# Turning matrices on the way through a DMA: gate and expert tiles of a two-layer graph kernel

## The chip, the core and the metric

The kernel runs on one core of one Trainium2 chip. The metric is the device time of one launch in microseconds (us), the median over several runs. The engines are called by what they do: TensorE (PE in the profile; its weight loads are PEld), VectorE (DVE), ScalarE (ACT), GpSimd (POOL) and SyncE (SP), which here only issues DMAs.

## The reference, cut to what matters

There are 128 graphs of 64 nodes, so 8192 tokens of 256 features, and two layers. Each layer is a graph step and then a mixture of experts, each with a layer norm ahead and a residual sum behind. The change touches the mixture of layer 0 alone:

```python
H = jax.nn.gelu(xf @ W1 + b1, approximate=False)        # 8192 x 1024
probs = jax.nn.softmax((H @ Wg + bg) / TEMP, axis=-1)   # 8 experts
assign = jnp.argmax(probs, axis=-1)
for e in range(Wd.shape[0]):                            # Wd[e]: 1024 x 256
    y = H @ Wd[e] + bd[e]
    out = out + jnp.where(assign == e, probs[:, e] * y, 0.0)
```

So each token needs the product with one of eight matrices, that of its best expert. Layer 1 holds an attention over each graph, a second mixture of four experts and a gate that is computed over a graph of 1,048,576 edges.

## The kernel before

Tokens stand in 64 tiles of 128 and in 16 groups of four tiles (`GR = 4`, 512 tokens). Three stages of layer 0 matter here.

**The gate.** `gated(g)` works on one group. It normalises the four tiles (`z`, L734), turns them on TensorE (L746, evicted by ScalarE at L747), and then `hidden` makes eight tiles hT of 128 hidden features x 512 tokens: two matmuls (L498) and a gelu on ScalarE (L501) each. hT has features on the partitions. The logits come from hT by a further product (L765, L769, L774); softmax, best expert and the rank of each token within its expert's list are small VectorE operations. The token's place is `pos` = expert x 8192 + rank.

To sort the tokens by expert, their gelu rows must go to `hrows` in device memory, one row of 1024 floats for each token. So each hT is turned back by four transposes on TensorE (`turned`, L755) and copied by ScalarE into `rows` (L756), which has tokens on the partitions; this runs `BEHIND = 4` steps after the gelu. At the end of the group four indirect DMAs on GpSimd's queue (L818) scatter the rows, 128 rows of 4 KB each. `rows` is a single buffer; hT tiles come from the pool `bh` with ten buffers.

**The early tiles.** `early_slots` works on 8 tiles of 128 sorted rows that are complete before the gate ends. Each is loaded from `hrows` (L900, two DMAs of 256 KB), turned by eight transposes (L911) and copied (L913), multiplied with its expert's `wd` (L932), and stored.

**The slots.** `slots` works through 60 such tiles. For each: a load of 512 KB (`hin`, L1238, two tiles ahead), eight transposes (L1247) and two copies on ScalarE (L1250) into `hTt`, eight products (L1265) that sum into one PSUM tile, the bias on VectorE (L1273), and a store to `yrows` (L1274). The expert's number is read from a table into registers, and picks `wd` and the bias row.

What runs beside them sets the order. The instruction streams of a part (two groups) are mixed by `mix` in the proportion of their steps, and each engine then has one fixed order of instructions. Beside the gate run the graph step of the groups ahead (L645 to L693) and, on VectorE, `keys.collect`: 16 chunks of the edge list, each loaded by SP (L279), searched for its largest keys by repeated max and replace (L296, L297), and written back by SP (L316). Source, destination and key tiles of a chunk have one buffer each. Beside the slots run on VectorE the later part of that sorting (`steps`, L373 to L451) and the counting of edges (`counts`: comparisons at L203, matmuls at L341), and `back_early`, which gathers finished rows on GpSimd's queue (L1193). All plain loads and stores of these stages are issued by SP, whose queue is in order.

Of the kernel before, what the change touches and what calls it, by code (L numbers as in the profile page):

```python
# [10 lines left out]
F32 = mybir.dt.float32  # L11
I32 = mybir.dt.int32
U32 = mybir.dt.uint32
U8 = mybir.dt.uint8
BF16 = mybir.dt.bfloat16
# [19 lines left out]
EARLY = 8  # L35
BACKED = 3 * PART
# [33 lines left out]
BEHIND = 4  # L70
# [14 lines left out]
def kernel(  # L85
# [102 lines left out]
    hrows = dram.tile([E0 * N, FD], F32, name="hrows")  # L188
    yrows = dram.tile([(NSLOT + EARLY) * P, D], F32, name="yrows")
    psel = const.tile([P, NT], F32, name="psel")  # L190
    row_y = const.tile([P, NT], I32, name="row_y")
    off = const.tile([P, NT, 64], U8, name="off")
    cnt = const.tile([P, NT], F32, name="cnt")
# [261 lines left out]
    with tc.tile_pool(name="w0", bufs=1, reuse_waits="tile") as w0, tc.tile_pool(name="kp", bufs=1, reuse_waits="tile") as kp:  # L455
# [15 lines left out]
        slot_e = w0.tile([P, NSLOT], I32, name="slot_e")  # L471
        slot_row = w0.tile([P, NSLOT], I32, name="slot_row")
# [13 lines left out]
        with tc.tile_pool(name="bg1", bufs=1, reuse_waits="tile") as bg1, tc.tile_pool(  # L486
# [19 lines left out]
            with tc.tile_pool(name="b2", bufs=1, reuse_waits="tile") as b2, tc.tile_pool(  # L506
# [199 lines left out]
                of_row = bg1.tile([P, 1], I32, name="of_row")  # L706
                nc.gpsimd.iota(of_row, pattern=[[0, 1]], base=0, channel_multiplier=1)
# [17 lines left out]
                def gated(g):  # L725
# [24 lines left out]
                    rows = b2.tile([P, GR, FD], F32, name="rows")  # L750

                    def turned(q):
                        th = psb.tile([P, GR * P], F32, name="tz")
                        for k in range(GR):
                            nc.tensor.transpose(th[:, k * P : k * P + P], hTs[q][:, k * P : k * P + P], ident)  # L755
                        S.copy(rows[:, :, q * P : q * P + P], th.rearrange("p (k n) -> p k n", k=GR))  # L756

                    for q, _ in enumerate(hidden(zT, hTs)):
                        if q >= BEHIND:
                            turned(q - BEHIND)  # L760
                        yield
# [8 lines left out]
                    turned(NH - BEHIND)  # L770
# [4 lines left out]
                    turned(NH - BEHIND + 1)  # L775
# [8 lines left out]
                    turned(NH - BEHIND + 2)  # L784
# [10 lines left out]
                    turned(NH - BEHIND + 3)  # L795
# [19 lines left out]
                    for k in range(GR):  # L815
                        t = GR * g + k
                        alone(
                            nc.gpsimd.indirect_dma_start(  # L818
                                hrows, bass.IndirectOffsetOnAxis(ap=pos[:, t : t + 1], axis=0), rows[:, k, :], None
                            )  # L820
                        )
# [55 lines left out]
                def early_slots():  # L877

                    _, rows_at = nc.values_load_multi_w_load_instructions(
                        early_row,  # L880
                        engines=(mybir.EngineType.SP,),
                        min_val=0,
                        max_val=E0 * N - P,
                        skip_runtime_bounds_check_because=why,
                    )
                    _, ex = nc.values_load_multi_w_load_instructions(
                        early_e,
                        engines=(mybir.EngineType.SP, mybir.EngineType.PE),
                        min_val=0,
                        max_val=E0 - 1,  # L890
                        skip_runtime_bounds_check_because=why,
                    )
                    loaded, turned_ = {}, {}

                    def load(t):

                        loaded[t] = []
                        for i in range(0, FD, GR * P):
                            h = bh.tile([P, GR * P], F32, name="hT")
                            got = nc.sync.dma_start(h, hrows[bass.ds(rows_at[t], P), i : i + GR * P])  # L900
                            for other in sends[-PART * GR :]:
                                tc.declare_no_dep(got.ins, other, reason="rows of an early tile were sent before")
                            loaded[t].append(h)

                    def turn(t):

                        turned_[t] = []
                        for h in loaded.pop(t):
                            th = psb.tile([P, GR * P], F32, name="tz")
                            for k in range(GR):  # L910
                                nc.tensor.transpose(th[:, k * P : k * P + P], h[:, k * P : k * P + P], ident)  # L911
                            hT = bh.tile([P, GR * P], F32, name="hT")
                            S.copy(hT, th)  # L913
                            turned_[t].append(hT)

                    load(0)
                    load(1)
                    turn(0)
                    yield
                    for t in range(EARLY):  # L920
                        if t + 2 < EARLY:
                            load(t + 2)
                        if t + 2 == EARLY:
                            y_last = bh.tile([P, GR * P], F32, name="hT")[:, 0:D]
                        if t + 1 < EARLY:
                            turn(t + 1)
                        hT = turned_.pop(t)
                        bd = b2.tile([P, D], F32, name=f"z{2 + t % 2}")
                        nc.sync.dma_start(bd, f0_bd[bass.ds(ex[t], 1), :].to_broadcast([P, D]))
                        py = psb.tile([P, GR * P], F32, name="ph")[:, 0:D]  # L930
                        for q in range(NH):
                            nc.tensor.matmul(  # L932
                                py,
                                hT[q // GR][:, q % GR * P : q % GR * P + P],
                                wd[:, bass.ds(ex[t], 1), q, :].rearrange("p e f -> p (e f)"),
                                start=(q == 0),
                                stop=(q == NH - 1),
                            )
                        y = y_last if t == EARLY - 1 else b2.tile([P, D], F32, name=f"z{t % 2}")
                        V.tensor_tensor(y, py, bd, ALU.add)  # L940
                        queue = nc.sync if t < EARLY - 2 else nc.gpsimd
                        queue.dma_start(yrows[(NSLOT + t) * P : (NSLOT + t + 1) * P, :], y)
                        yield
# [10 lines left out]
                for i in range(n_parts + 2):  # L954
# [18 lines left out]
                    if i == 1:  # L973
                        with tc.issue_after(first_made[-1]):
                            for e in range(E0):
                                nc.sync.dma_start(
                                    hrows[e * N : e * N + P, :].rearrange("p (k f) -> p k f", f=P),
                                    none.unsqueeze(1).to_broadcast([P, FD // P, P]),
# [177 lines left out]
        if True:  # L1156
            with tc.tile_pool(name="bs", bufs=3, reuse_waits="tile") as bs, tc.tile_pool(
                name="bt", bufs=2, reuse_waits="tile"
            ) as bt, tc.tile_pool(name="be", bufs=2, reuse_waits="tile") as be, tc.tile_pool(name="bz", bufs=3, reuse_waits="tile") as bz, tc.tile_pool(
                name="psy", bufs=2, space=PSUM, reuse_waits="tile"  # L1160
            ) as psy, tc.tile_pool(name="pst", bufs=4, space=PSUM, reuse_waits="tile") as pst, ExitStack() as of_keys:
# [44 lines left out]
                def slots(first, end):  # L1206

                    found, loaded, turned = {}, {}, {}

                    def load(t):  # L1210

                        if t % GR == 0:
# [10 lines left out]
                                engines=(mybir.EngineType.SP, mybir.EngineType.PE),  # L1223
# [6 lines left out]
                                engines=(mybir.EngineType.SP,),  # L1230
# [6 lines left out]
                        h = loaded[t] = bz.tile([P, FD], F32, name="hin")  # L1237
                        nc.sync.dma_start(h, hrows[bass.ds(found[t][0], P), :])  # L1238

                    def turn(t):  # L1240

                        h = loaded.pop(t)
                        hT = turned[t] = bt.tile([P, NH, P], F32, name="hTt")
                        for i in range(0, NH, GR):
                            th = pst.tile([P, GR * P], F32, name="th")
                            for k in range(GR):
                                nc.tensor.transpose(  # L1247
                                    th[:, k * P : k * P + P], h[:, (i + k) * P : (i + k) * P + P], ident
                                )
                            S.copy(hT[:, i : i + GR, :].rearrange("p q n -> p (q n)"), th)  # L1250

                    for t in range(first, min(first + 2, end)):
                        load(t)
                    turn(first)
                    for t in range(first, end):
                        if t + 2 < end:
                            load(t + 2)
                        if t + 1 < end:
                            turn(t + 1)
                        (_, e, to), hT = found.pop(t), turned.pop(t)  # L1260
                        bd = bs.tile([P, D], F32, name="bd")
                        nc.sync.dma_start(bd, f0_bd[bass.ds(e, 1), :].to_broadcast([P, D]))
# [11 lines left out]
                        stored = nc.sync.dma_start(yrows[bass.ds(to, P), :], y)  # L1274
# [1209 lines left out]
```

## Time and profile before

| | |
|---|---|
| median of 15 runs | 2006.2 us (1998.43 to 2014.45) |
| the profiled execution | 2005.77 us |
| its span in the profile | 2004.0 us |
| busy: TensorE / VectorE / ScalarE / GpSimd | 1874.6 / 1354.3 / 949.1 / 454.1 us |
| mean granted TensorE clock | 0.983 |
| DMA: moved, mean rate | 284.91 MB, 142 GB/s |

The span runs from the first to the last record of the profile; the time of the execution is 1.8 us longer. A busy share is an average over stages with different limits, so the table of stages in the prediction counts for more than this one. Float32 matmuls are recorded as several instructions each (960 for the 480 products of the slots), and overlap: the busy time of a group is the time that it covers, which is less than its number times its mean length.

### The profile page before, as it was taken

To read this page: it belongs to the slowest core of one execution; us is meant where nothing else is said; L and a number is where in the kernel's file an instruction comes from. 1 tells how busy PE (TensorE), PEld (TensorE's weight loads), DVE (VectorE), ACT (ScalarE), POOL (GpSimd) and SP (SyncE) were. 2 spreads that over 40 slices of the span, in tenths; PEclk is the share of its full clock that TensorE was granted. 3 is DMA by queue.
4 is the path that set the end of the run, shared out by engine and by line. 5 is a ranking of instruction groups with operands and counts; after the bars stand their busy time and mean duration, and the time that the engine had idled before them with its cause. 6 is when DMAs were issued, how large, how long until landed. Compare 5 with 4: busy or idle time off the path is not lost. (4 is left out here: it accounts for less than half of the span.)

```text
span 2004.0 us, 32697 instructions
## 1 busy us (share of the span) xinstructions
PE 1874.6 (94%) x10609; PEld 1329.8 (66%) x10609; DVE 1354.3 (68%) x4535; ACT 949.1 (47%) x1740; POOL 454.1 (23%) x467
## 2 busy tenths in 40 slices
PE   7888989989999999999978999999999989999999
PEld 5444544444557888888646666656666658888876
DVE  6789988972456899998498656847778443234435
ACT  4867667676663222122567766323333323333332
POOL 3010111011111011120231100016666543312223
PEclk9999999999999999999979999999999999999999
DMA  9752322323425555455224211662222358888833
GB/s 295 204 166 83 119 83 100 105 87 115 147 82 177 174 181 175 156 175 165 61 69 143 68 51 55 203 169 57 59 54 60 90 179 286 279 252 272 278 119 95
DMA packets 243552, 284.91 MB, mean 142 GB/s; under 512 B 55920, under 2 KB 195312, under 8 KB 243376
## 3 DMA queue, kind: packets, MB, share of 16 engines
q1 hardware_dynamic: 209392, 221.96, 35.9%
q0 software_dynamic: 23136, 60.48, 9.4%
q8 instruction: 89, 1.46, 0.3%
q10 hardware_dynamic: 10848, 0.30, 0.3%
q14 instruction: 87, 0.71, 0.1%
HBM read 159.40 MB, written 123.18 MB: 141 GB/s over the span
## 5 line engine op out<-in xcount | busy, mean ns | idle before, releaser
L498 PE MATMUL ph<-zT,w 128*128 128x512 f32 x512 | 250.3, 610 | 6.0 <-ACT zT L747 4.9
L1265 PE MATMUL py<-wd,hTt 128*128 x960 | 217.9, 380 | 0.7 <-ACT hTt L1250 0.7
L1878 POOL DMA_INDIRECT got<-tsrc,esrc x144 | 156.9, 1090 | 174.4 <-DVE esrc L1849 77.3
L1265 PEld LDWEIGHTS py<-wd,hTt 128*128 128x128 f32 x960 | 178.5, 191 | 22.9 <-ACT hTt L1250 0.9
L1415 PE MATMUL py<-w,hT 128*128 128x256 f32 x736 | 175.4, 390 | 8.7 <-DVE td L2237 4.9
L1250 ACT COPY hTt<-th 128x512 f32<-128x512 f32 x120 | 64.4, 589 | 240.2 <-PE th L1247 227.4
L1405 PE MATMUL ph<-zT,w 128*128 128x512 f32 x368 | 169.9, 604 | 1.3 <-issue 1.2
L1415 PEld LDWEIGHTS py<-w,hT 128*128 128x128 f32 x736 | 139.0, 194 | 36.5 <-issue 12.1
L498 PEld LDWEIGHTS ph<-zT,w 128*128 128x128 f32 x512 | 92.6, 194 | 98.5 <-issue 79.5
L2363 ACT ACTIVATE hT<-ph,b1e 128x256 f32<-128x256 f32 x152 | 72.1, 474 | 179.2 <-PE ph L2359 98.0
L1409 ACT ACTIVATE hT<-ph,b 128x512 f32<-128x512 f32 x92 | 63.1, 688 | 171.1 <-PE ph L1405 135.4
L2359 PE MATMUL ph<-zTp,w1e 128*128 128x256 f32 x608 | 140.0, 384 | 4.4 <-DMA w1e<-in_L_ffn_W_dram 4.4
L818 POOL DMA_INDIRECT hrows<-rows,pos x64 | 64.7, 1011 | 338.2 <-issue 185.5
L2380 DVE TENSOR_TENSOR y<-py,b2e 128x256 f32<-128x256 f32 x76 | 32.3, 424 | 160.6 <-PE py L2372 149.2
L2372 PE MATMUL py<-w,hT 128*128 x608 | 137.8, 379 | 1.7 <-issue 1.7
L2359 PEld LDWEIGHTS ph<-zTp,w1e 128*128 128x128 f32 x608 | 117.2, 193 | 21.0 <-issue 4.6
L501 ACT ACTIVATE hT<-ph,b 128x512 f32<-128x512 f32 x128 | 88.1, 688 | 83.5 <-PE ph L498 75.4
L660 PE MATMUL pre<-wd 128*128 128x512 f32 x256 | 124.5, 604 | 1.9 <-ACT wd L646 1.3
L2372 PEld LDWEIGHTS py<-w,hT 128*128 128x128 f32 x608 | 112.6, 190 | 15.8 <-issue 2.1
L1405 PEld LDWEIGHTS ph<-zT,w 128*128 128x128 f32 x368 | 67.8, 191 | 69.4 <-issue 68.6
L2393 POOL DMA_INDIRECT back<-yslots,place x64 | 64.3, 1005 | 169.3 <-ACT hT L1409 49.3
L755 PEld LDWEIGHTS tz<-ident,hT 128*128 128x128 f32 x512 | 62.2, 143 | 53.4 <-issue 42.0
(499 smaller groups left out, 3881.8 us busy)
## 6 DMA issues: line engine op xcount, KB each, us to landing
hin<-hrows SPq DMA_DIRECT2D x60, 512.0 KB
w1e<-in_L_ffn_W_dram SPq DMA_DIRECT2D x38, 512.0 KB
yin<-ystore SPq DMA_DIRECT2D x24, 512.0 KB
yrows<-none SPq DMA_DIRECT2D x10, 1024.0 KB
zslots<-none SPq DMA_DIRECT2D x38, 256.0 KB
zin<-zslots SPq DMA_DIRECT2D x38, 256.0 KB
yslots<-y SPq DMA_DIRECT2D x76, 128.0 KB
ystore<-y SPq DMA_DIRECT2D x72, 128.0 KB
```

The costliest lines, as they stand in the source:

```text
L498: nc.tensor.matmul(ph, w1[:, c, q * P : q * P + P], zT[:, c, :], start=(c == 0), stop=(c == 1))
L501: gelus.append(S.activation(hT, ph, AF.Gelu, bias=b1[:, q : q + 1]).ins)
L660: nc.tensor.matmul(pre, xnT[:, c, n * P : n * P + P], wcat[:, c, :], start=(c == 0), stop=(c == 1),)
L818: nc.gpsimd.indirect_dma_start(hrows, bass.IndirectOffsetOnAxis(ap=pos[:, t : t + 1], axis=0), rows[:, k, :], None)
L1250: S.copy(hT[:, i : i + GR, :].rearrange("p q n -> p (q n)"), th)
L1265: nc.tensor.matmul(py, hT[:, q, :], wd[:, bass.ds(e, 1), q, :].rearrange("p e f -> p (e f)"), start=(q == 0), stop=(q == NH - 1),)
L1405: nc.tensor.matmul(ph, w1[:, e, c, q * P : q * P + P], zT[:, c, :], start=(c == 0), stop=(c == 1))
L1415: nc.tensor.matmul(py, hTs[q][:, k * P : k * P + P], w2[:, e, q, :], start=(q == 0), stop=(q == NH1 - 1))
L1878: nc.gpsimd.indirect_dma_start(got, None, tsrc, bass.IndirectOffsetOnAxis(ap=esrc[:, b, at : at + 1], axis=0))
L2359: nc.tensor.matmul(ph, w1e[:, c, q * P : q * P + P], zT[:, c, :], start=(c == 0), stop=(c == 1))
L2363: pace[:] = [S, S.activation(hT, ph, AF.Gelu, bias=b1e[:, q : q + 1]).ins]
L2372: nc.tensor.matmul(py, hTs[q][:, k * P : k * P + P], w2[:, e, q, :].rearrange("p e f -> p (e f)"), start=(q == 0), stop=(q == NH1 - 1),)
```

## The change

The turns leave TensorE and ScalarE and become transposing DMAs on SP's queue. Such a DMA takes two-byte elements, so a row of floats is handled as two rows: one of the lower halves of its 1024 floats, one of the upper halves, 2 KB each. `hrows` has twice as many rows of 1024 two-byte elements. In the gate a transposing DMA (128 x 1024 two-byte elements, 256 KB) takes each hT as soon as its gelu is done to `rows`, in which each partition now holds half rows. Half row number 2 x place + (0 or 1) must be known on the partition that holds it: two small matmuls with a matrix that spreads 64 tokens over 128 partitions, and one VectorE operation, make that index. The sends become eight per group with 2 KB rows instead of four with 4 KB rows. Early tiles and slots are loaded by a transposing DMA from `hrows` straight into the layout that the products need: two of 256 KB for an early tile, one of 512 KB for a slot, now three slots ahead (`AHEAD = 3`). Bias loads and result stores of these two stages move from SP's queue (and for the last two early tiles from GpSimd's) to ScalarE's queue. The PSUM tiles that held the turns are gone; `py` gets four buffers instead of two.

```diff
-    hrows = dram.tile([E0 * N, FD], F32, name="hrows")
+    hrows = dram.tile([E0 * N * 2, FD], U16, name="hrows")
...
-                    rows = b2.tile([P, GR, FD], F32, name="rows")
-
-                    def turned(q):
-                        th = psb.tile([P, GR * P], F32, name="tz")
-                        for k in range(GR):
-                            nc.tensor.transpose(th[:, k * P : k * P + P], hTs[q][:, k * P : k * P + P], ident)
-                        S.copy(rows[:, :, q * P : q * P + P], th.rearrange("p (k n) -> p k n", k=GR))
+                    rows = b2.tile([P, 2 * GR, FD], U16, name="rows")
 
                     for q, _ in enumerate(hidden(zT, hTs)):
-                        if q >= BEHIND:
-                            turned(q - BEHIND)
+                        nc.sync.dma_start_transpose(rows[:, :, q * P : q * P + P], hTs[q].bitcast(U16))
                         yield
...
-                    for k in range(GR):
-                        t = GR * g + k
+                    p2 = psg0.tile([P, GR * P], F32, name="ms")[:, 0 : 2 * GR].rearrange("p (k h) -> p k h", h=2)
+                    for j in range(2):
+                        nc.tensor.matmul(p2[:, :, j], spread_pos[j], m, start=True, stop=True)
+                    at = pr.rearrange("p k e -> p (k e)")[:, 0 : 2 * GR].bitcast(I32)
+                    V.tensor_scalar(at, p2.rearrange("p k h -> p (k h)"), 2.0, odd, ALU.mult, ALU.add)
+                    yield
+                    for j in range(2 * GR):
                         alone(
                             nc.gpsimd.indirect_dma_start(
-                                hrows, bass.IndirectOffsetOnAxis(ap=pos[:, t : t + 1], axis=0), rows[:, k, :], None
+                                hrows, bass.IndirectOffsetOnAxis(ap=at[:, j : j + 1], axis=0), rows[:, j, :], None
                             )
                         )
...
-                            got = nc.sync.dma_start(h, hrows[bass.ds(rows_at[t], P), i : i + GR * P])
-                            for other in sends[-PART * GR :]:
+                            got = nc.sync.dma_start_transpose(
+                                h.bitcast(U16).rearrange("p (q r) -> p q r", q=GR),
+                                hrows[bass.ds(rows_at[t] * 2, 2 * P), i : i + GR * P],
+                            )
+                            for other in sends[-PART * GR * 2 :]:
...
-                        nc.sync.dma_start(bd, f0_bd[bass.ds(ex[t], 1), :].to_broadcast([P, D]))
+                        nc.scalar.dma_start(bd, f0_bd[bass.ds(ex[t], 1), :].to_broadcast([P, D]))
...
-                        queue = nc.sync if t < EARLY - 2 else nc.gpsimd
-                        queue.dma_start(yrows[(NSLOT + t) * P : (NSLOT + t + 1) * P, :], y)
+                        nc.scalar.dma_start(yrows[(NSLOT + t) * P : (NSLOT + t + 1) * P, :], y)
...
-                        h = loaded[t] = bz.tile([P, FD], F32, name="hin")
-                        nc.sync.dma_start(h, hrows[bass.ds(found[t][0], P), :])
...
+                        hT = loaded[t] = bt.tile([P, NH, P], F32, name="hTt")
+                        nc.sync.dma_start_transpose(
+                            hT.rearrange("p q r -> p (q r)").bitcast(U16).rearrange("p (q r) -> p q r", q=NH),
+                            hrows[bass.ds(found[t][0] * 2, 2 * P), :],
+                        )
+
+                    def bias(t):
+
+                        bd = biases[t] = bs.tile([P, D], F32, name="bd")
+                        nc.scalar.dma_start(bd, f0_bd[bass.ds(found[t][1], 1), :].to_broadcast([P, D]))
...
                         y = bs.tile([P, D], F32, name="y")
                         add_bd = V.tensor_tensor(y, py, bd, ALU.add).ins
-                        stored = nc.sync.dma_start(yrows[bass.ds(to, P), :], y)
+                        stored = nc.scalar.dma_start(yrows[bass.ds(to, P), :], y)
```

## The prediction

> **What bounds the kernel now.** I read the busy shares first, then a table of the stages that the change touches, then groups and waits, then the DMA queues. The stage borders are the starts of z (L734) on ScalarE, two groups to a row: 70.7 to 619.7 us is the gate of layer 0 (16 groups), 619.7 to 663 the early tiles, 663 to 966.5 the 60 slots. Columns: length, busy us (instructions) by engine, granted clock, DMA share, GB/s.
>
> ```profile
> core 0: us, PE busy (x) PEld busy (x) DVE busy (x) ACT busy (x) POOL busy (x), PEclk, DMA share, GB/s
> 70.70:141.60 70.90, 61.37 (x229) 32.63 (x229) 62.16 (x218) 51.44 (x90) 5.36 (x6) 0.95 0.65 195
> 212.20:283.60 71.40, 66.35 (x285) 35.81 (x284) 64.43 (x239) 51.49 (x89) 10.03 (x12) 1.00 0.28 96
> 431.80:498.60 66.80, 61.98 (x261) 33.07 (x261) 21.42 (x92) 47.49 (x81) 8.78 (x8) 1.00 0.28 95
> 498.60:555.70 57.10, 53.49 (x316) 29.56 (x316) 24.97 (x100) 36.88 (x61) 8.11 (x8) 1.00 0.42 148
> 619.70:663.00 43.30, 40.44 (x325) 34.74 (x324) 34.22 (x154) 8.99 (x17) 4.97 (x6) 1.00 0.57 183
> 663.00:966.50 303.50, 299.46 (x2593) 268.03 (x2593) 268.94 (x683) 64.44 (x120) 39.34 (x25) 0.99 0.53 168
> ```
>
> TensorE is the bound everywhere, at 0.92 of the time in the gate and 0.99 in the slots. But VectorE is right behind it (64 of 71 us; 269 of 303.5), until its edge chunks run out near 440 us: what TensorE saves, VectorE may keep.
>
> ```profile
> L1265 PE MATMUL py<-wd,hTt 128*128 x960 | 217.9, 380 | 0.7 <-ACT hTt L1250 0.7
> L1250 ACT COPY hTt<-th 128x512 f32<-128x512 f32 x120 | 64.4, 589 | 240.2 <-PE th L1247 227.4
> L755 PE MATMUL tz<-ident,hT x512: 272/273/331, 94.9 to 617.9; 128*128 128x128 f32 x171
> L1247 PE MATMUL th<-ident,hin x480: 272/273/451, 663.1 to 959.3; 128*128 128x128 f32 x160
> ```
>
> These are the turns. One takes 273 ns, but they overlap: asked for alone, L755 covers 78.96 us (154 ns each) and L1247 64.96 us (135 ns).
>
> ```profile
> SPq L316 <- DVE key L314: 114.4, 9, 17.5
> DVE key L283 <- DMA left<-key: 14.3, 9, 3.4
> L818 POOL DMA_INDIRECT hrows<-rows,pos x64: 957/964/1507, 128.8 to 630.6; - x64
> ```
>
> SP's queue waits for VectorE's chunks, up to 17.5 us at a time, and VectorE waits for SP's left stores: `key` has one buffer.
>
> ```profile
> q1 hardware_dynamic: 209392, 221.96, 35.9%
> q10 hardware_dynamic: 10848, 0.30, 0.3%
> ```
>
> No row shows a transposing DMA; these two give its bounds.
>
> **The price of a transposing DMA (T, for 256 KB).** At the least, the plain rate: the slots move 168 GB/s at a share of 0.53, so 317 GB/s when full, T = 0.83 us. At the most, the rate of the smallest packets: 0.3% of 16 engines over 2004 us is 96 us for 10,848 packets, 8.9 ns for 28 bytes, 50 GB/s over 16 engines, T = 5.2 us. Between: q1's packets take 55 ns for 1060 bytes (35.9% x 16 x 2004 / 209,392). A line through both points gives 19 ns for 256 bytes, which is one block of 128 two-byte elements, the run that both sides of this transfer have; 1024 of these on 16 engines are T = 1.2 us. I take 1.2, as the nearest by run length, and 2.4 us for the 512 KB of a slot. The Trainium skill, "DMA: Bandwidth & Descriptors", Latency and other measured facts, gives 261 GB/s for a DMA transpose with a non-contiguous middle dimension; by that T would be 1.0 us and the sum below about 6 us lower (estimate). Against the change speaks "VectorE: DVE Perf Modes", The three transpose paths: 1309 ns by DMA for 128x128 two-byte elements against 390 on TensorE; were that a rate and not one transfer's latency, T would be 8 x 1.309 = 10.5 us and the kernel would take some 4200 us (estimate). No run here shows either yet.
>
> **Gate.** Removed: 512 transposes, 79.0 us of TensorE, and 128 copies into rows, 74.0 us of ScalarE (L756). Added: 128 transposing DMAs on SP, 64 more sends on POOL (128 of half the size), and per group two small matmuls and one small VectorE operation (a 128x4 to 128x32 operation takes 0.17 us: under 0.5 us per group in all, hidden in the idle tenth).
>
> Groups 0 and 1 (70.9 us): the DMA share is 0.65 and VectorE has 62 us; I give them 4. Groups 2 to 11 take 357.0 us. TensorE: their windows hold 326.6 us, less 48.7 of turns, so 27.8 per group; at today's fill of 0.91, 30.5. VectorE: the instruction order puts 13 edge chunks between groups 1 and 11 where before they lay between 1 and 9. A chunk is 15.3 us in the timeline (348.66 to 364.4 less one foreign operation), other work 9 per group: (13 x 15.3 + 10 x 9) / 10 = 28.9, at the same fill 31.7. I take 31.2 per group, 312 us: **45 less**. Groups 12 to 15 have little VectorE work; the copies of their gate logits on ScalarE (L769) lie 29.3, 25.4, 25.4 and 28.3 us apart, 108.4. Here a new loop binds. `rows` has one buffer, and the first transposing DMA of a group waits until all eight sends of the group before have landed. Sends start 1.27 us apart on POOL: 10.2 us; a landing is about 2.8 us (the left store that VectorE waits for, 345.8 to 348.7); then 8T, and a landing again: 15.8 + 8T, 25.4 us at T = 1.2. So 102 instead of 108: I take **8 less**, with the overlap of the last landing. In groups 2 to 11 the same loop hides under 31.2 us while T is under 1.9.
>
> SP now carries the transposing DMAs between edge loads and left stores. If one waits for a chunk (17.5 us at worst), the ones behind it wait; hT has 10 buffers and a group uses 9, so TensorE has a group's slack, and what is late is the sends, which have 5.8 us per group. The other way round, a transposing DMA that waits for sends holds a left store, and VectorE stands. Gate: 57 less.
>
> **Early tiles.** 64 transposes (L911), 135 ns each, 8.7 us, and 16 copies go; the loads run two tiles ahead, as before. Products of 28 us and counts of 4.8 us stay. I take 5 of the 8.7, since the eight last sends now end 5 us later on POOL, beside it.
>
> **Slots.** 65 us of TensorE and all 64.4 of ScalarE go: TensorE has 234.5 left, VectorE still 268.9. So VectorE takes over; 25 of its 34.6 idle us waited for TensorE (23.1 and 2.2 ahead of L1273). At 0.96 busy: 280 us, **23 less** (35 at most, at no idle time; nothing, if the two keep waiting for each other through the counts). A load is one transposing DMA, three ahead; per slot the DMA engines have 0.53 x 5.06 = 2.7 us of work, of which a plain load is 1.65; with 2.4 it is 3.4 of 4.7 us. It would bind from 3.6 us a load (T = 1.8). The bias loads and stores move to ScalarE's queue: two issues at 0.33 us (the median of SP's hin issue), and a store waits there for VectorE's addition, but behind it stand only the next bias load and store, as ScalarE has nothing else in this stage. SP is relieved of two issues of three.
>
> **Sum.** 57 + 5 + 23 = 85 less. The profiled execution took 2005.8 us (span 2004.0), 0.4 below the median: 1920.7, and by the median 1921. I say 1920.
>
> **Rivals.**
> 1. The turn moves into the DMA engines and is dearer there than it was on TensorE. For: nothing in the trace shows that a crossbar keeps up with plain copies, and elements are two bytes. Against: runs of 256 bytes, and DMA shares of 0.28 and 0.53 leave room. It decides from T of about 2.1 us (125 GB/s): a slot then takes 1.05 + 4.2 = 5.25 us, 315 in all, 11 more; the gate's loop is 32.6 us, 31 less in groups 2 to 11 and 22 more in groups 12 to 15: even. At T = 3 the loop is 39.8 us, 16 times 637 instead of 549, and the slots 7.05 us, 423 instead of 303.5: about 2215 with the early tiles. At T = 5.2 the same working gives 918, 687 and 83: 2800 us.
> 2. VectorE and SP's order give most of it back. For: VectorE is at 0.9 in both stages, and stands today for up to 3.4 us at a left store. If all 13 chunks meet such a wait behind a transposing DMA, 44 of the 85 are gone: 1965. Against: the chunks are spread wider now, and where VectorE is the bound, SP's other work comes early.
> 3. The turns are wholly hidden today: then within 4 us of 2006. Against: TensorE at 0.99 in the slots waits for nobody.
>
> **Numbers.** A measurement here tells a change of about 0.2%, 4 us, from none. Likeliest case 0.55: 1885 to 1950 alone (T from 0.83 to 1.9, VectorE between 0.93 and full). Rival 2, 0.13: 1950 to 2000. Rival 3, 0.02. Rival 1, 0.30, of which 0.12 up to 2110 (T to about 2.6) and the rest far above. So faster 0.68, same 0.02, slower 0.30; leaving out 0.03 below and 0.17 above, the range is 1885 to 2110.
>
> **What would show it.** Right: no L755, L756, L1247, L1250; groups 2 to 11 near 31 us apart by z, VectorE over 0.9 there; the slots near 280 us with VectorE at 0.95 and TensorE at 0.83, ScalarE empty. SP's transposing issues not waiting long for anything but gelu and sends. Wrong: TensorE waiting for the hTt load by DMA in the slots (rival 1), DMA share near full there; gate groups at equal distance given by sends and landing (the loop); VectorE's waits for left over 40 us (rival 2).

## The result, and the profile after

The changed kernel takes 2036.21 us (median of 12 runs, 2027.37 to 2042.99) against 2007.21 us for the kernel before (62 runs): a ratio of 1.0139, 95% interval 1.0124 to 1.0154. It is slower by 29 us by these medians, where 85 less were forecast. The chips differ by about 1.5% in their absolute times, so every experiment below is given as a ratio to the kernel before on the same chip.

The first view is again the table of stages, with the borders where the same events lie after the change: groups 0–1, 4–5, 10–11, 12–13, then the hand-over (from the copy of group 15's logits to the first work of TensorE on an early tile, which is now a product and was a turn), the early tiles, the slots. Columns: length, busy us (instructions) by engine, granted clock, DMA share, GB/s.

```profile
core 0: us, PE busy (x) PEld busy (x) DVE busy (x) ACT busy (x) POOL busy (x), PEclk, DMA share, GB/s
71.10:136.30 65.20, 53.91 (x185) 27.94 (x185) 53.63 (x192) 46.49 (x81) 8.18 (x9) 0.95 0.85 227
218.30:291.60 73.30, 62.95 (x229) 32.24 (x228) 60.20 (x232) 44.67 (x74) 18.72 (x21) 0.93 0.58 149
446.50:520.50 74.00, 60.35 (x213) 30.21 (x212) 57.91 (x222) 40.42 (x65) 16.43 (x17) 0.91 0.70 186
520.50:575.80 55.30, 50.26 (x259) 26.16 (x258) 28.78 (x116) 29.03 (x45) 12.02 (x14) 0.91 0.85 217
633.10:658.30 25.20, 5.40 (x79) 4.80 (x75) 10.87 (x37) 2.17 (x3) 3.30 (x4) 0.55 0.82 155
658.30:712.70 54.40, 36.98 (x217) 29.75 (x217) 31.73 (x149) 0.00 (x0) 7.74 (x8) 0.88 0.99 169
712.70:990.70 278.00, 256.35 (x2113) 221.76 (x2113) 255.99 (x659) 0.00 (x0) 30.48 (x24) 0.98 0.92 181
```

Neither TensorE (0.82 to 0.86) nor VectorE (0.78 to 0.82) is full any more in groups 4–5 and 10–11: the gate waits. The granted clock there is 0.91 to 0.93, where it was 1.00. The hand-over is a hole of 25 us with 5.4 us of matmul in it; before it was 4.6 us long (614.9 to 619.5). The slots came out as forecast, ScalarE empty.

The turns are gone, and their price is readable from SP's issues of the two lines (duration of an issue, min/median/max ns):

```profile
L763 SPq DMA_TRANSPOSE rows<-hT x128: 1232/1326/4099, 86.8 to 652.1; - x128
L1232 SPq DMA_TRANSPOSE hTt<-hrows x60: 1307/2354/5362, 705.6 to 974.6; - x60
```

Of the groups, the slots' products; TensorE stands 7.5 us for a load by DMA, and does so once:

```profile
L1253 PE MATMUL py<-wd,hTt 128*128 x960 | 227.2, 391 | 7.5 <-DMA hTt<-hrows 7.5
```

The DMA queues (packets, MB, share of 16 engines): q1, SP's, has more than twice the packets (209,392 before) for 16 MB more.

```profile
q1 hardware_dynamic: 456016, 237.96, 47.5%
q10 hardware_dynamic: 30432, 18.14, 3.7%
```

The list of waits (70 to 640 us), with the two lines that answer to those shown of before:

```profile
DVE key L284 <- DMA left<-key: 74.4, 13, 10.7
SPq L763 <- DMA hrows<-rows,pr: 100.9, 26, 18.1
SPq L317 <- DVE key L315: 57.5, 4, 21.5
```

VectorE's wait for the left store went from 14.3 to 74.4 us. SP waits 100.9 us for sends at the new transposing DMAs. How one makes the other is seen in the timeline around 270 us (start, duration, what; idle time before it in brackets). SP:

```profile
258.18 10.90 SPq L763 DMA_TRANSPOSE rows<-hT  x8
269.18 0.53 SPq L317 DMA_DIRECT2D left<-key  x1
295.45 5.40 SPq L763 DMA_TRANSPOSE rows<-hT  x4
```

GpSimd, the first send of each of two groups:

```profile
244.53 0.99 POOL L822 DMA_INDIRECT hrows<-rows,pr  x1 [20.63 <-DVE guess L157]
283.20 0.96 POOL L822 DMA_INDIRECT hrows<-rows,pr  x1 [28.24 <-DVE pr L818]
```

VectorE:

```profile
265.15 0.42 DVE L691 SCALAR_TENSOR_TENSOR x<-pre,x 128x256 f32<-128x256 f32 x1
271.99 0.43 DVE L284 TENSOR_SCALAR key<-src 128x512 f32<-128x512 int32 x1 [6.42 <-DMA left<-key]
273.06 0.18 DVE L784 TENSOR_REDUCE psum<-pr 128x4 f32<-128x32 f32 x1
282.70 0.22 DVE L818 TENSOR_SCALAR pr<-ms,of_row 128x8 int32<-128x8 f32 x1 [0.55 <-PE ms L816]
```

Read it as a loop. A group's sends start at 244.5; the next group's eight transposing DMAs need `rows` free and start at 258.2; the left store stands behind them on SP until 269.2; VectorE cannot begin the next chunk before that store has landed (272.0), and the softmax of the group just turned stands behind the chunk's first operation; its half-row indices are made at 282.7; only then do its sends start, at 283.2, and the next transposing DMAs at 295.5: 37.3 us after the last.

At the end of the gate, SP again:

```profile
641.14 12.19 SPq L763 DMA_TRANSPOSE rows<-hT  x8
654.95 19.77 SPq L904 DMA_TRANSPOSE hT<-hrows  x11
```

The early tiles' loads (L904) come after group 15's transposing DMAs, and those waited 18.1 us for group 14's sends.

### The profile page after: what moved, and what is told of

Its sections match the earlier page's. It is cut to its first block, busy times and chain, and to the rows that moved or that the text cites. A ratio compares the mean times of both kernels' runs of the same rounds, so it can differ in the third digit from the quotient of the medians.

```text
span 2030.5 us, 30848 instructions
## 1 busy us (share of the span) xinstructions
PE 1799.3 (89%) x9617; PEld 1247.1 (61%) x9617; DVE 1343.6 (66%) x4555; ACT 816.3 (40%) x1476; POOL 503.5 (25%) x529
## 5 line engine op out<-in xcount | busy, mean ns | idle before, releaser
L504 PE MATMUL ph<-zT,w 128*128 128x512 f32 x512 | 262.1, 639 | 5.5 <-ACT zT L757 2.9
L822 POOL DMA_INDIRECT hrows<-rows,pr x128 | 126.7, 990 | 493.3 <-DVE pr L818 246.9
L1253 PE MATMUL py<-wd,hTt 128*128 x960 | 227.2, 391 | 7.5 <-DMA hTt<-hrows 7.5
L1253 PEld LDWEIGHTS py<-wd,hTt 128*128 128x128 f32 x960 | 181.4, 194 | 33.2 <-issue 9.8
L1361 ACT ACTIVATE z<-x,fac 128x256 f32<-128x256 f32 x64 | 34.1, 595 | 354.1 <-SPq L1317 354.0
L1393 PE MATMUL ph<-zT,w 128*128 128x512 f32 x368 | 168.1, 599 | 0.0
L504 PEld LDWEIGHTS ph<-zT,w 128*128 128x128 f32 x512 | 97.7, 204 | 94.9 <-issue 81.8
L2360 PEld LDWEIGHTS py<-w,hT 128*128 128x128 f32 x608 | 112.6, 190 | 14.5 <-issue 0.8
L1393 PEld LDWEIGHTS ph<-zT,w 128*128 128x128 f32 x368 | 67.2, 190 | 66.9 <-issue 66.0
L1187 POOL DMA_INDIRECT yearly<-yrows,cnt x24 | 30.5, 1270 | 245.7 <-DVE x L1178 93.9
## 6 DMA issues: line engine op xcount, KB each, us to landing
zslots<-none SPq DMA_DIRECT2D x38, 256.0 KB
zin<-zslots SPq DMA_DIRECT2D x38, 256.0 KB
```

The source lines that it names most:

```text
L504: nc.tensor.matmul(ph, w1[:, c, q * P : q * P + P], zT[:, c, :], start=(c == 0), stop=(c == 1))
L822: nc.gpsimd.indirect_dma_start(hrows, bass.IndirectOffsetOnAxis(ap=at[:, j : j + 1], axis=0), rows[:, j, :], None)
L1253: nc.tensor.matmul(py, hT[:, q, :], wd[:, bass.ds(e, 1), q, :].rearrange("p e f -> p (e f)"), start=(q == 0), stop=(q == NH - 1),)
L1393: nc.tensor.matmul(ph, w1[:, e, c, q * P : q * P + P], zT[:, c, :], start=(c == 0), stop=(c == 1))
L2360: nc.tensor.matmul(py, hTs[q][:, k * P : k * P + P], w2[:, e, q, :].rearrange("p e f -> p (e f)"), start=(q == 0), stop=(q == NH1 - 1),)
```

## The experiments

**1. The left store leaves SP's queue.** The loop above says that the store is the link between the transposing DMAs and VectorE.

```diff
-            nc.sync.dma_start(
+            nc.gpsimd.dma_start(
                 left[c * n_chunk : c * n_chunk + n_chunk].rearrange("n p e -> p n e"),
```

> The changed kernel with one edit: the 16 left stores of the edge chunks go out on GpSimd's queue instead of SP's. Theory A (the ring: eight transposing DMAs wait on SP for the sends, the left store stands behind them, VectorE stands at its one key buffer for it, and the softmax chain behind that on VectorE makes the next sends late): the groups 2 to 11 fall from 38.4 us apart to 30 to 33, VectorE's wait for left from 74 us to under 25, and the time to 1940 to 1985. Rival B (the loop of one rows buffer alone, sends, landing, eight transposing DMAs, landing, is the bound, or the transposing DMAs are too slow): the spacing stays over 36 us and the time within 15 us of 2036. Rival C (VectorE simply is full): the same as B, with VectorE busy over 0.95 in the gate.

Measured: ratio 0.9958 (0.9933 to 0.9982), and once more on another chip 0.9962 (0.9949 to 0.9975): nearly 2% under the changed kernel, and 0.4% faster than the kernel before. Groups 1 to 11 are 34.5 us apart by their logits copies (38.3 after, 35.7 before). VectorE's wait for the store fell to this (the same view, 70 to 620 us):

```profile
DVE key L284 <- DMA left<-key: 29.9, 9, 5.6
```

So the link is shown. But the wait stayed above the 25 us that I had expected, the spacing above 30 to 33 us, and the time (1992 us) above 1985: something else holds the gate too.

> The left store on GpSimd's queue once more, on the same chip as the two runs beside it, as their base: ratio to before 0.993 to 0.999.

**2. The edge loads too.** L280's two loads also go to GpSimd's queue.

```diff
-                nc.sync.dma_start(t, ev[k, :, c * CHUNK : c * CHUNK + CHUNK])
+                nc.gpsimd.dma_start(t, ev[k, :, c * CHUNK : c * CHUNK + CHUNK])
```

> The same as e1, and the 32 edge loads go out on GpSimd's queue as well, so that in the gate SP carries almost nothing but transposing DMAs. Theory A: some 0 to 10 us below e1, as the loads too stood behind transposing DMAs (but a GpSimd queue that waits for VectorE holds them now). Rival B and C: no change from 2036.

Measured: 1.0023 (1.0003 to 1.0044), worse than the store alone. Waits for the store rose to 44.7 us: GpSimd's queue now waits 61.4 us for VectorE's `key` at these loads, ahead of sends. I read this as the same blockade on another queue; how long the sends themselves stood behind the loads I have not traced.

**3. The store stays on SP, but nobody waits for it.** Odd chunks take their key tile from unused room in `wd`.

```diff
-            keys = self.work.tile([P, CHUNK + PER], F32, name="key")
+            keys = self.spare if c % 2 else self.work.tile([P, CHUNK + PER], F32, name="key")
...
+                keys.spare = carve(CHUNK + PER)
```

> The changed kernel with a second buffer for the key tile of an edge chunk (odd chunks use the spare end of wd's space); all queues as in the changed kernel. Theory A: VectorE no longer stands for the left store, its wait for left falls from 74 us to under 15, the sends come earlier, and groups 2 to 11 fall from 38.3 us apart (by the copies of the logits) to 32 to 35; the time is 1965 to 1995, no worse than with the left stores on GpSimd's queue (1992). If the left store was not the link, the spacing stays over 37 and the time over 2025.

Measured: 1.0001 (0.9987 to 1.0015), 1.4% under the changed kernel. The wait for the store is all but gone; what took its place is the next thing in SP's queue (waits, 130 to 488 us):

```profile
DVE wd L284 <- DMA src<-in_L_ffn_edge_index_dram: 16.1, 3, 8.5
DVE src L289 <- DMA dst<-in_L_ffn_edge_index_dram: 7.2, 2, 4.4
```

Now VectorE waits for edge loads, which stand on SP where the left store stood. Spacing 35.7 us, where 32 to 35 were expected.

**4. Both.** Two key buffers and the store on GpSimd's queue.

> The two key buffers, and the left store on GpSimd's queue as well. Theory A (the left wait and SP's order are one link, which either edit breaks): once VectorE no longer waits for the left store, moving the store off SP's queue brings little more, since what SP waits for is the sends (102 us of its waits at L763's transposing DMAs) and what VectorE waits for is the edge loads behind those; ratio to before 0.992 to 1.002, spacing of the gate's groups 34.5 to 36 us. Theory B (two separate losses that add up: the left store also holds SP's queue while it waits for VectorE's reduction): the two gains add, spacing 32 to 33.5 us and a ratio of 0.975 to 0.988.

Measured: 0.9979 (0.9958 to 1.0), spacing 35.6 us. The two gains do not add; they are one link, broken in two ways.

**5. What the sends cost.** With two key buffers, each send is issued twice, the second time to another tensor.

```diff
                         alone(
                             nc.gpsimd.indirect_dma_start(
                                 hrows, bass.IndirectOffsetOnAxis(ap=at[:, j : j + 1], axis=0), rows[:, j, :], None
                             )
                         )
+                        twice(
+                            nc.gpsimd.indirect_dma_start(
+                                hagain, bass.IndirectOffsetOnAxis(ap=at[:, j : j + 1], axis=0), rows[:, j, :], None
+                            )
+                        )
```

> As e5, but every send is issued twice, the second time to another tensor in device memory, so that a group has sixteen sends of 1.27 us instead of eight. Theory A (what is left is the ring over the one rows buffer: sends, landing, transposing DMAs, logits and rank, sends): each group takes about 10 us longer, 130 to 165 us in all, as GpSimd's 10 us lie in the ring. Rival (TensorE or VectorE is the bound and the sends lie beside them, GpSimd being a quarter busy): within 20 us of e5.

Measured in a single execution: a span of 2026.8 against 1976.6 us, 50 more, where I had expected 130 or more. Groups 1 to 11 are only 1.1 us further apart (36.9), the last four 9.6 us (34.5 instead of 24.9). So the loop over the single `rows` buffer sets the pace in the last four groups, where VectorE has no chunks left, and hides in the others once the left store is out of it. There the doubled sends also exhaust the gelu buffers: `ACT hT L508 <- DMA rows<-hT` is 57.2 us in the waits.

**6. What taking the turns off TensorE was worth.** On top of experiment 1, each hT is turned on TensorE as before, with nobody reading the result.

```diff
+                    def turned(q):
+                        th = psb.tile([P, GR * P], F32, name="tz")
+                        for k in range(GR):
+                            nc.tensor.transpose(th[:, k * P : k * P + P], hTs[q][:, k * P : k * P + P], ident)
+
                     for q, _ in enumerate(hidden(zT, hTs)):
+                        if q >= BEHIND:
+                            turned(q - BEHIND)
                         nc.sync.dma_start_transpose(rows[:, :, q * P : q * P + P], hTs[q].bitcast(U16))
```

(and the last four at the places where they stood before).

> The left store on GpSimd's queue; and each gelu block is turned on TensorE as well, as before, with nobody reading the result (no ScalarE copy): the 512 transposes are back as dead work, to price what taking them off TensorE was worth. Theory A (TensorE is not the bound of the gate any more, the ring of sends, softmax and transposing DMAs and VectorE's order are): spacing within 1 us of 34.5, granted clock of the gate up from 0.94 towards 1.00, ratio within 0.004 of the run beside it. Theory B (TensorE with its waits is the bound): 10 groups x 4.9 us of covered time come back in part, 15 to 45 us, ratio 1.003 to 1.02.

Measured: 1.0049 (1.0036 to 1.0062) against 0.9962 on the same chip, 17 us; spacing 36.9 instead of 34.6 us. The windows of groups 1 to 11, experiment 1 first, then with the dead turns:

```profile
145.00:491.00 346.00, 302.43 (x1110) 153.89 (x1111) 277.39 (x1065) 216.95 (x353) 94.78 (x101) 0.95 0.65 162
```

```profile
145.00:514.00 369.00, 337.54 (x1428) 186.31 (x1428) 279.86 (x1065) 217.67 (x352) 93.78 (x101) 0.96 0.64 155
```

Without the turns TensorE covers 35 us less and these ten groups take 23 us less; over the whole program 17 us remain. So 17 us is what taking the turns off TensorE was worth, once the store was moved. The run doesn't show what bounds the gate without them, where TensorE covers 0.87 of the time and VectorE 0.80. Nor does it price the clock, which is nearly the same in both (0.95 and 0.96).

**7. The gate turned on TensorE, early tiles and slots by DMA.** The eight half-row sends stay; each turn is copied by ScalarE in two strided copies of two-byte elements.

```diff
+                        halves = th.bitcast(U16).rearrange("p (k n h) -> p k h n", k=GR, h=2)
+                        for h in range(2):
+                            S.copy(rows[:, :, h, q * P : q * P + P], halves[:, :, h, :])
```

> The gate's half of the change undone: TensorE turns the gelu values as before, and ScalarE copies them into half rows (two copies of 128x512 two-byte elements for each turn instead of one of 128x512 floats, so ScalarE has some 75 us more over the gate, beside its idle third); early tiles and slots keep their transposing loads. Theory A: the loss lies in the gate, so this is faster than before by what slots and early tiles bring: 1970 to 1995, with the slots at 275 to 285 us. Rival B in the form that transposing loads cost in the slots: 2005 to 2030.

A miss: 1.0222 (1.0182 to 1.0262), slower than the changed kernel. Groups (130 to 640 us):

```profile
L769 ACT COPY rows<-tz 128x512 uint16<-128x512 uint16 x214 | 115.0, 603 | 53.1 <-DMA hrows<-rows,pr 43.0 <-PE tz L766 10.0
```

Waits:

```profile
PEld tz L766 <- ACT rows L769: 32.8, 23, 5.2
```

The split into halves makes 16 copies of 0.6 us per group of what were eight, ScalarE waits 43 us for sends to free `rows`, and TensorE waits for ScalarE. This variant therefore does not undo the gate's part cleanly: it prices half rows without transposing DMAs, and shows only that they are no cheap middle way. Two stages of it answer other questions: its slots, with their transposing loads, took 278.9 us, so Rival B falls; and its first early product follows the logits copy of group 15 by 4.1 us.

**8. Slots without the 60 bias loads.** With two key buffers; one bias row, loaded once, is added for all slots.

> As e5, but the 60 bias loads of the slots are left out: one bias row, loaded once, serves all slots (in these inputs all bias rows are zero, so the sum is the same). Tells what bounds the slots now, where VectorE shows 0.97 and the DMA engines 0.98. If VectorE: the slots stay at 273 to 280 us, and the time within 6 us of e5. If the DMA engines: they lose about a tenth of their work there, and the slots fall to 245 to 260 us.

The slots' windows, with the bias loads and without:

```profile
678.10:955.20 277.10, 256.02 (x2113) 221.58 (x2113) 256.13 (x659) 0.00 (x0) 30.90 (x24) 0.98 0.91 181
```

```profile
674.90:951.30 276.40, 257.53 (x2113) 222.80 (x2113) 255.62 (x660) 0.00 (x0) 31.22 (x24) 0.97 0.74 155
```

DMA share 0.74 instead of 0.91, and the stage is 0.7 us shorter. The DMA engines do not bound the slots. The ratio is 0.9969 (0.9957 to 0.9982) against 1.0001 with the loads, so nearly all of the gain came from outside this stage: in the two profiles the early tiles are 5.7 us shorter (48.7 and 54.4) and what follows the slots 6.2. Why is open.

**9. The hand-over: which queue?** With two key buffers, group 15's eight transposing DMAs alone go out on ScalarE's queue.

```diff
+                        queue = nc.scalar if g == NG - 1 else nc.sync
-                        nc.sync.dma_start_transpose(rows[:, :, q * P : q * P + P], hTs[q].bitcast(U16))
+                        queue.dma_start_transpose(rows[:, :, q * P : q * P + P], hTs[q].bitcast(U16))
```

> The two key buffers, and group 15's eight transposing DMAs alone go out on ScalarE's queue in place of SP's. Theory A (the hand-over's 20 us is SP's order: the early tiles' loads stand behind group 15's transposing DMAs, which wait for group 14's sends): the first early load leaves SP 8 to 16 us earlier against the logits copy of group 15, the time from that copy to the first early product falls from 27 us (two key buffers) to 12 to 18, and the ratio to before is 0.004 to 0.007 under that of the two key buffers alone. Theory B (the loads wait for the gelu buffers that those transposing DMAs read, on whichever queue they are): hand-over within 4 us of 27 and no change. Theory C (ScalarE is held by its own eight issues, some 11 us, and the softmax of group 15 with its sends comes as much later): sends of group 15 move back 8 us or more.

> Two key buffers, left store on GpSimd's queue, group 15's transposing DMAs on ScalarE's queue. Theory A: ratio to before 0.987 to 0.997, the sum of the two runs beside it. If the hand-over edit does nothing, it is that of the two key buffers with the left store on GpSimd's queue.

Measured: 0.9988 (0.997 to 1.0006), and with the store on GpSimd's queue 0.9983 (0.9963 to 1.0004): no gain that can be told from experiments 3 and 4. The first early product does follow the logits copy of group 15 by 8.5 us instead of 27.1, but only because ScalarE, held by its own issues, which wait for group 14's sends, makes that copy as much later. SP's waits in the latter run (585 to 660 us) say why:

```profile
SPq L907 <- DMA rows<-hT: 27.1, 2, 26.1
```

L907 are the early loads. On another queue than group 15's transposing DMAs, they still wait for them. That looks like Theory B, but the trace doesn't show it to be the buffers: the first of these loads, which fills one buffer, waits for the semaphores of all eight transposing DMAs on ScalarE's queue. In the changed kernel and in experiment 4 it waits for those of TensorE and of a bias load, and for the eight only by the order of SP's queue. So here the program put a wait between the two queues that is not one for a single buffer, and the run can't tell Theory A from Theory B. C is half right: the copy comes later, but the last send of group 15 stays where it was, 71.7 us after the logits copy of group 14 (70.5 in experiment 4).

**10. The hand-over: which buffers?** With experiment 1's store, the loads of early tiles 0 and 1 go to other places and are issued ahead of group 15's transposing DMAs and sends.

```diff
+                        if t == 0:
+                            places = b2.tile([P, 2, GR * P], F32, name="zT")
+                        if t == 1:
+                            places = w1[:, 1, :].rearrange("p (c f) -> p c f", c=2)
...
-                            h = bh.tile([P, GR * P], F32, name="hT")
+                            h = places[:, i // (GR * P), :] if t < 2 else bh.tile([P, GR * P], F32, name="hT")
...
                     load(0)
                     load(1)
+                    ((hTs, rows, at),) = last
+                    for q in range(NH):
+                        nc.sync.dma_start_transpose(rows[:, :, q * P : q * P + P], hTs[q].bitcast(U16))
```

> The left store on GpSimd's queue; and at the end of the gate the four transposing loads of early tiles 0 and 1 are issued on SP ahead of group 15's eight transposing DMAs, into zT's place and a half of w1, which are free by then, in place of four of group 15's gelu buffers. Theory A (the hand-over waits for the gelu buffers of group 15, which its own transposing DMAs hold while they wait for group 14's sends): with another place the loads are on the way before the logits copy of group 15, the first early product follows that copy by 5 to 14 us in place of 25.7, the early tiles' end comes 10 to 18 us earlier, and the ratio to before is 0.984 to 0.991. Theory B (group 15's sends and the early tiles' later loads, which still stand behind the transposing DMAs, are the real end): the first product comes earlier, but tile 2 waits as long as tile 0 did, and the ratio stays within 0.002 of the run beside it.

Measured: 0.9934 (0.9921 to 0.9947) against 0.9962 for experiment 1 on the same chip, 7 us by the medians (1962.66 and 1969.92): the fastest version of this study. Its timeline of the early products on TensorE:

```profile
597.48 1.53 PE L948 MATMUL ph<-wd,zT 128*128 x6
...
609.68 0.68 PE L948 MATMUL ph<-wd,w 128*128 x2
622.48 3.59 PE L948 MATMUL ph<-wd,hT 128*128 x8 [11.42 <-DMA hT<-hrows]
```

The first product follows the logits copy (594.7) by 2.7 us instead of 26.6. Then tile 2 waits 11.4 us, as its load still stands behind group 15's transposing DMAs, and the last early product ends at 656.3 us in both runs; only the first product of the slots comes 5.8 us earlier (661.0 and 666.8). Each theory gets a half: tiles 0 and 1 did wait behind group 15's transposing DMAs, and all of that comes back by the last early product. The edit gives the loads other buffers and an earlier place on SP's queue at once, so which of the two held them stays open.

## Why the prediction was wrong

Forecast 1920, measured 2036. By stages of the two profiles, after minus before:

| term | forecast | measured |
|---|---|---|
| groups 0 and 1 | -4 | -5.7 (65.2 - 70.9) |
| groups 2 to 11, by z | -45 | +27.2 (384.2 - 357.0) |
| groups 12 to 15, to the last logits copy | -8 | -3.7 (112.6 - 116.3) |
| hand-over to the early tiles | 0 | +20.6 (25.2 - 4.6) |
| early tiles | -5 | +10.9 (54.4 - 43.5) |
| slots | -23 | -25.5 (278.0 - 303.5) |
| the rest | 0 | +2.7 |

They sum to 26.5 us, the difference of the spans.

**Right in the number, by luck in part: the slots.** 280 us forecast, 278.0 measured. But I had VectorE alone as the bound, at 0.96 of the stage (268.9 us) and TensorE at 0.83 (234.5 us). Both are at 0.92 (256.0 and 256.4 us): TensorE's cover fell by 43 us, not 65, and VectorE's by 13, not 0.

**Right: the loop of the last four groups.** Sends, landing, eight transposing DMAs, landing: 102 us forecast for groups 12 to 15; their logits copies span 103.9, where they spanned 108.3 before. Experiment 5 shows that this loop sets their pace.

**Right in kind, small in size: T.** Forecast 1.2 us. Issued, a 256 KB transposing DMA takes 1.33 us on SP, eight in a row 10.9 us. On the DMA engines a slot's load is dearer: with two key buffers, between 750 and 900 us, q1 has 67.8% of the engines' time over 33 such loads (and one store of 256 KB), 3.08 us each at full engines, 1.54 for 256 KB, or 24 ns for each of its packets where my line through two points gave 19 (an estimate, as the other queues' share lies beside it). In the slots that was no matter, as experiment 8 shows. Rival 1 did not happen. The rate of that load is 512 KB in 3.08 us, 170 GB/s; the 261 GB/s of "DMA: Bandwidth & Descriptors", Latency and other measured facts, in the Trainium skill was not reached here. The 1309 ns that "VectorE: DVE Perf Modes", The three transpose paths, gives for 128x128 by DMA is about what an issue of eight times that size took here (1326 ns), so read as a rate it would have misled.

**The step that failed: groups 2 to 11.** My loop was sends, landing, eight transposing DMAs, landing: 15.8 + 8T, and I let it hide under 31.2 us. Two things were left out of it. First, SP's left store behind the transposing DMAs and, through `key`'s single buffer, VectorE with the softmax behind it; with them the loop is the 37.3 us shown above, which hides under nothing. I named this link in a sentence ("a transposing DMA that waits for sends holds a left store, and VectorE stands") and gave it no price in the sum, only in Rival 2. Rival 2's signature came: waits for `left` over 40 us. Its price there, 44 us, is near what the store's move brought back, about 1.8% or 36 us. Its share of what it "gives back" was right; that the rest of the 85 us was there to be kept was not.

Second, I took 48.7 us of turns off TensorE's 326.6 us at the old fill: the time that the turns cover when they are asked for alone.

```profile
141.60:498.60 357.00, 326.57 (x1389) 176.11 (x1388) 281.40 (x1059) 253.54 (x433) 44.58 (x50) 1.00 0.29 99
134.30:482.00 347.70, 303.02 (x1117) 154.46 (x1116) 283.83 (x1086) 216.71 (x353) 95.32 (x105) 0.95 0.65 163
```

These are groups 2 to 11 by z, before and in experiment 1 (its second chip). Worked out from the records of before, TensorE's cover there without L755 is 301.1 us: other matmuls ran in 23 of the 48.7, and only 25 were there to be taken from the cover. Experiment 1 kept 303.0, so 30.3 per group and not 27.8, at a fill of 0.87 where I had kept 0.91. So even with the store moved, the groups are 34.5 us apart by the logits copies (34.8 by z) and not 31.2. The same step is wrong in the slots: L1247 covers 65.0 us alone, but without it 253.4 of the 299.5 us that TensorE covers there remain. Why the fill fell stays open; the granted clock was lower too (0.95 for 1.00; L504's mean is 626 ns there, L498's was 602), but no run prices it.

**Not in the sum at all: the hand-over.** I costed only the last sends. The transposing DMAs hold group 15's gelu buffers and SP's queue until the sends of the group before have freed `rows`, and the early loads stand behind them. Experiment 7, which has no transposing DMA in the gate but keeps those of the early tiles, has a hand-over of 4.1 us, and experiment 10 one of 2.7; so group 15's transposing DMAs are the wait. Whether they hold it by their place on the queue or by the buffers, experiments 9 and 10 do not separate; the semaphores of the changed kernel speak for the queue, at least for the first load. "The loads run two tiles ahead, as before" was the wrong sentence.

**Early tiles.** TensorE's cover fell from 40.6 to 37.0 us and the stage grew by 10.9, at a DMA share of 0.99. The last 7.5 of it are the wait ahead of the first slot's product (L1253 above): that load leaves SP at 705.64 and the product starts at 712.75, where before the first slots' loads were issued at 657.80, 5 us ahead of the first turn. TensorE's other waits there are for VectorE, 9.9 us where they were 1.3, and VectorE itself waits 8.2 us for bias loads, which it did not do before; what made it late beyond that I have not traced.

**Rival 3** is refuted as a whole by the slots; in the gate, experiment 6 leaves it no more than a part.

## What to carry to other kernels

When work moves from a compute engine into a DMA queue, write down for that queue what stands behind each new entry and what each entry waits for, and follow it until the loop closes: here it closed over a store, a single buffer and another engine's softmax, and the loop's length, not any busy share, was the time. Do the same at the hand-over to the next stage, for the queue and for the buffers that the last DMAs still read: here it grew from 4.6 to 25.2 us. And take the gain of removed engine work from what that engine covers without it, not from what the removed instructions cover by themselves: here 25 us in ten groups, not 49.

## What the runs showed of the hardware that I had not expected

The granted TensorE clock in the gate, two groups at a time, was 0.95 to 1.00 before, at a cover of 0.87 to 0.95, and 0.88 to 0.95 after, at a cover of 0.77 to 0.93; in the hand-over it was 0.55 at a cover of 0.21. With the dead turns back it was 0.96 in groups 1 to 11 and 1.00 between 485 and 600 us. Clock and cover fell together, but no run here tells which follows which: a cover of 0.90 had a clock of 1.00 before, and one of 0.91 a clock of 0.91 after. A DMA share of 0.91 to 0.92 over the slots was no bound: taking it to 0.74 (experiment 8) left the stage within 0.7 us of what it was.
